# Two small matrix products of a two-layer graph kernel computed in column halves of the TensorE array

## The chip, the cores and the metric

The kernel runs on one core of one Trainium2 chip. A core has a matrix engine (TensorE, PE in the profile, with its weight loads shown apart as PEld), a vector engine (VectorE, DVE), a scalar engine (ScalarE, ACT), GpSimd (POOL) and a queue engine for transfers (SyncE, SP). TensorE writes its results to PSUM, the other operands lie in SBUF. The metric is the device time of the whole launch in microseconds (us), as the median of three runs; lower is better.

## What is computed

The input is a batch of eight graphs with 2048 nodes and 256 features each, and one adjacency matrix for all of them. Layer 0 is attention by chunks of 256 nodes with four heads of 64 features, in which every chunk has its own softmax; its output product (`ctx @ Wo.T`) goes through two residuals and two layer norms. Layer 1 is a graph attention whose values are the product of layer 0's result with `W`. The reference, cut:

```python
q = (x @ Wq.T + bq).reshape(B, N, H, Dh).transpose(0, 2, 1, 3)   # k, v likewise
scores = jnp.einsum('bhnd,bhjcd->bhnjc', q, kc) / sqrt(Dh)
scores = jnp.where(mask == 0, -10.0, jnp.clip(scores, -10.0, 10.0))
attn = jax.nn.softmax(scores, axis=-1)
ctx = jnp.einsum('bhnjc,bhjcd->bhnd', attn, vc)
out = layernorm(ctx @ Wo.T + bo + x) * gamma + beta
x = _layernorm(x + out)
...
Wh = (h @ W).reshape(B, N, N_H, D_F)
e = s_src[:, :, None, :] + s_dst[:, None, :, :]
e = jnp.where(mask, jnp.where(e > 0, e, 0.2 * e), -jnp.inf)
alpha = softmax(e, axis=2)
h_out = elu(jnp.einsum('bijh,bjhd->bihd', alpha, Wh))
x = _layernorm(x + h_out)
```

All matrix products of the layers are in float32.

## The kernel before

The graphs are worked through one after the other (`b` from 0 to 7), and the two layers are interleaved: while layer 0 of graph `b` is computed, layer 1 of graph `b - 1` runs beside it. The order of the instructions on every engine is the order in which the program issues them; nothing moves them later.

Layer 0 of a graph is cut into 64 slots (`SLOTS`). A slot is one group of 512 query nodes (`q`, four of them), one pair of heads (`hp`) and one chunk of keys (`c`). For TensorE a slot of the middle graphs is a fixed sequence:

- `scores` of the next slot (L388, tile `ps`): queries by keys, with 64 rows of the array for one head and the other 64 rows for the second, in the profile 64*128.
- `product(s, 0)` (L425, tile `pc`): probabilities by values for the first head. The 128 query nodes of a tile are cut into two halves of 64, `z` = 0 and 1, each of which takes 64 columns of the array and 64 partitions of PSUM, in the profile 128*64.
- `lower.step()` (L761, tile `pa`): two tiles of layer 1 of the graph before, cut the same way, 128*64.
- `product(s, 1)` (L425, tile `pc`): the second head.

A float32 matrix product shows as two records in the trace, each with a weight load of its own.

Class `Between` carries a group of 512 nodes from layer 0 to layer 1. Its `output` (L531, matmuls in L540, tile `po`) multiplies the attention result, which lies turned in `qT`, with `wo_sb`: for every tile of 128 nodes two matmuls, one for each half of the 256 inner features, with all 128 columns of the array, in the profile 128*128. Its `values` (L576, matmuls in L581, tile `pw`) multiplies the turned result of layer 0, `x1T`, with `w1_sb`, whose rows hold 256 values and eight attention terms, in the same way. DVE takes `po` from PSUM in `add` (L551), ACT takes `pw` in two copies (L588, L592). The steps between them are the norms on DVE, ACT and POOL.

Tables (`BEHIND`, `WIDE_BEHIND`, `LATER_BEHIND`) name the slots of a group behind which `output` and `values` are issued, with two tiles of nodes at a time: after `product(s, 1)`, and so before the next slot's `scores`. A graph has three groups in its slots, with two calls of `output` each and five calls of `values` together (the third group's second call falls behind the slots); the last of the five follows slot 63. The fourth group follows after the slots, at the change of layers: `order` is written out by hand there. For the first seven graphs it interleaves the group's steps with the projections of the next graph (L332 `pp`, L348 `pv`, 128*128) and the end of the third group's values, `before.values((2, 3))`. For the last graph there is no next one, and the steps stand between steps of layer 1 (`lower.step`). After that layer 1 of the last graph runs alone.

Other names in the views: `pr` (L399 on DVE, L411 on ACT) are the masked scores and their exponentials, `e` (L739, DVE) the attention weights of layer 1, `raw` (L432, ACT) the copy of `pc` out of PSUM, `pm` (L249) transposes of the mask in the first graph.

Of the kernel before, what the change touches and what calls it, by code (L numbers as in the profile page):

```python
# [17 lines left out]
P = 128  # L18
# [4 lines left out]
def adj_resnorm_kernel(  # L23
# [19 lines left out]
    nc = tc.nc  # L43
    B, N, F = x.shape
    H, D = a_src.shape
    NT = N // P
    NCH = N // CH
    KC = F // P
# [13 lines left out]

    SQ = 32
    QS = HP * NK
    SLOTS = NCH * QS
    UNITS = [(m, h) for m in range(len(BANKS)) for h in range(H)]
    FIRST = [sum(BANKS[:m]) for m in range(len(BANKS))]
# [51 lines left out]
    qT = big.tile([P, KC, N], F32, tag="qT", name="qT")  # L119
# [36 lines left out]
    wo_sb = weights(woT, "wo_sb")  # L156
# [5 lines left out]
    w1_sb = consts.tile([P, KC, F + 2 * H], F32, tag="w1_sb", name="w1_sb")  # L162
# [351 lines left out]
    class Between:  # L514
# [13 lines left out]
            row = beta_sb.unsqueeze(1).to_broadcast([P, QT, F])  # L528
            nc.vector.tensor_add(self.r, self.r, row)

        def output(self, us):  # L531
            n = len(us)
            if n == QT:
                po = two_banks([P, QT, F], "po")
            else:
                po = psM.tile([P, 2, F], F32, tag="psM", name="po")
            for k, u in enumerate(us):
                t = QT * self.g + u
                for c in range(KC):
                    nc.tensor.matmul(  # L540
                        po[:, k, :],
                        lhsT=qT[:, c, t * P : (t + 1) * P],
                        rhs=wo_sb[:, c, :],
                        start=(c == 0),
                        stop=(c == KC - 1),
                    )
            self.po = po

        def add(self, us):
# [23 lines left out]
        def turn_all(self):  # L573
            self.x1T = transposed(self.y, "x1T")

        def values(self, us):  # L576
            n, t = len(us), QT * self.g + us[0]
            pw = two_banks([P, n, CH], "pw")
            for k, u in enumerate(us):
                for c in range(KC):  # L580
                    nc.tensor.matmul(  # L581
                        pw[:, k, : F + 2 * H],
                        lhsT=self.x1T[:, c, u * P : (u + 1) * P],
                        rhs=w1_sb[:, c, :],
                        start=(c == 0),
                        stop=(c == KC - 1),
                    )
            nc.scalar.copy(  # L588
                self.waug[:, t : t + n, :, :D],
                pw[:, :, :F].rearrange("p k (h d) -> p k h d", h=H),  # L590
            )
            nc.scalar.copy(  # L592
                self.sd[:, :, t : t + n], pw[:, :, F : F + 2 * H].rearrange("p k x -> p x k")
            )
# [361 lines left out]
    for b in range(B):  # L956
        waug = blocks.tile([P, NT, H, D1], F32, tag="waug", name="waug")
        sd = small.tile([P, 2 * H, NT], F32, tag="sd", name="sd", bufs=1)
        if b == 0:
            for s in range(3):  # L960
                load_slab(s)
            scores(0)
            for u in range(KT):
                exps(0, u)
        if lower:
            for _ in range(STEP):
                lower.make()
        closing = Closing(b - 2, CLOSING) if b > 1 else None
        if closing:
            closing.do(-1)  # L970
        group = None
        for s in range(SLOTS):
            q, hp, c = where[s]
            i = s % QS
            send()
            if s + 3 < SLOTS:
                load_slab(s + 3)
            if i == 0:
                before = group
                group = Between(b, q - 1, sd, waug) if q else None  # L980
                wide = 0 < q < NCH - 1
                ahead = {} if wide else AHEAD
                if wide:
                    beside, behind = WIDE_BESIDE, WIDE_BEHIND
                else:
                    beside, behind = BESIDE if b else BESIDE_0, BEHIND
                later_beside, after = (LATER_BESIDE, LATER_BEHIND) if q > 1 else ({}, {})
            if before and later_beside and i in LATER_AHEAD:
                LATER_AHEAD[i](before)
            if i == 1 and q:  # L990
                load_context(b, q - 1, 1)
            if i == QS // 2 + 1:
                load_context(b, q, 0)
            if group and i in ahead:
                ahead[i](group)
            if s == SLOTS - 3 and b + 1 < B:
                turns = [project(b + 1, g) for g in range(NCH)]
                turns[0].pop(0)()
            if s:
                normalize(s - 1)  # L1000
            if s + 1 < SLOTS:
                scores(s + 1)

            if s == SLOTS - 1 and b + 1 < B:
                turns[0].pop(0)()
            if i == 3 and q:
                turn_context(q - 1, 1)
            if i == QS // 2 + (6 if wide else 3):
                turn_context(q, 0)
            if before and i in later_beside:  # L1010
                later_beside[i](before)
            if group:
                for step in beside.get(i, ()):
                    step(group)
            elif closing:
                closing.do(s, behind=False)
            product(s, 0)
            if s + 1 < SLOTS:
                for u in range(KT):
                    exps(s + 1, u)  # L1020
            if lower:
                if b + 1 < B or s < SLOTS - LATE:
                    lower.step()
            elif masks.left():
                masks.step()
            if not lower:
                product(s, 1, one_bank)
            elif b + 1 < B or s < SLOTS - LATE:
                product(s, 1)
            else:  # L1030
                product(s, 1, spare_bank)

            if before and i in after:
                after[i](before)
            if i == 0 and q:
                send_context(b, q - 1, 1)
            if i == QS // 2:
                send_context(b, q, 0)
            if group and i in behind:
                behind[i](group)  # L1040
            elif closing and not q:
                closing.do(s, beside=False)
        normalize(SLOTS - 1)

        send()
        before = group
        gd, fs = factors(b, sd, waug)
        group = None
        every = tuple(range(QT))

        def begin():
            nonlocal group
            group = Between(b, NCH - 1, sd, waug)

        def ctx():
            context(NCH - 1, 1)

        steps = [
            lambda: group.bias(),
            lambda: group.output(every),  # L1060
            lambda: group.add(every),
            lambda: (group.shift(), group.a.stats(every)),
            lambda: group.a.apply(group.y),
            lambda: (group.scale(), group.again(), group.b2.stats(every)),
            lambda: group.finish(),
            lambda: group.turn_all(),
            lambda: group.values((0, 1)),
            lambda: group.values((2, 3)),
        ]
        if b + 1 < B:  # L1070
            (k0, v0, q0), (l1, t1, k1, v1, q1), (l2, t2, k2, v2, q2), (l3, t3, k3, v3, q3) = turns
            rest = [lambda: lower.rest(1)] if lower else []
            order = [begin, *rest, l1, *rest, lambda: before.values((2, 3))]
            order += [*rest, ctx, *rest, *rest, k0]
            order += [steps[0], t1, steps[1], v0, steps[2], steps[3], l2, k1, steps[4], q0]
            order += [steps[5], v1, t2, l3, steps[6], q1, steps[7], k2, steps[8], steps[9], t3, v2]
            order += [lambda: [load_slab(s) for s in range(3)], fs[0], q2, fs[1], k3, fs[2], v3]
            order += [lambda: scores(0), q3, lambda: [exps(0, u) for u in range(KT)]]
        else:

            step = lower.step
            order = [begin, lambda: before.values((2, 3)), steps[0], step, ctx, step, steps[1], step]
            order += [steps[2], step, steps[3], step, steps[4], step, steps[5], step, steps[6], step]
            order += [steps[7], step, steps[8], step, steps[9], step, fs[0], step, fs[1], step, fs[2]]
            order += [step] * 5
            assert sum(p is step for p in order) == LATE
        for piece in order:
            send()
            piece()
        send()  # L1090
        undone = lower.tail if lower else []
        lower = Layer1(b, gd, waug)
        lower.tail += undone
# [57 lines left out]
```

## Time and profile before

| What | Value |
|---|---|
| Time, median of 3 runs | 3769.13 us |
| Lowest and highest run | 3766.95 and 3769.89 us |
| Span of the profiled execution, first to last instruction | 3764.9 us |
| Mean granted TensorE clock in it | 0.993 |
| `po` matmuls (L540): records, mean of one | 512, 391 ns |
| `pw` matmuls (L581): records, mean of one | 512, 398 ns |
| `pc` matmuls (L425): records, mean of one | 32768, 224 ns |
| `pa` matmuls (L761): records, mean of one | 32768, 224 ns |
| `ps` matmuls (L388): records, mean of one | 4096, 617 ns |

For the profiled execution the span is the only time there is; it lies 2.1 us below the lowest of the three runs. The duration of one matmul record covers its whole way through the array, while the next ones have already started: 32768 records of 224 ns would be 7.3 ms one after another. What a group of matmuls costs is therefore read from the start of its first record to the start of what follows it.

### The profile page before, as it was taken

To read this page: it belongs to the slowest core of one execution; us is meant where nothing else is said; L and a number is where in the kernel's file an instruction comes from. 1 tells how busy PE (TensorE), PEld (TensorE's weight loads), DVE (VectorE), ACT (ScalarE), POOL (GpSimd) and SP (SyncE) were. 2 spreads that over 40 slices of the span, in tenths; PEclk is the share of its full clock that TensorE was granted. 3 is DMA by queue.
4 is the path that set the end of the run, shared out by engine and by line. 5 is a ranking of instruction groups with operands and counts; after the bars stand their busy time and mean duration, and the time that the engine had idled before them with its cause. 6 is when DMAs were issued, how large, how long until landed. Compare 5 with 4: busy or idle time off the path is not lost.

```text
span 3764.9 us, 159631 instructions
## 1 busy us (share of the span) xinstructions
PE 3655.7 (97%) x72100; PEld 2743.7 (73%) x72100; DVE 3138.5 (83%) x4213; ACT 1979.9 (53%) x3571; POOL 1368.3 (36%) x1202
## 2 busy tenths in 40 slices
PE   9999999999999999999999999999999999999787
PEld 5656677776777777776777767777677777776676
DVE  5877589976999689995999959998699977997899
ACT  4666455555555555554555545555555555555322
POOL 1445234333433343333443324433343333334300
PEclk9999999999999999999999999999999999999899
DMA  6653334333333343333433334333433333332344
GB/s 164 152 117 70 80 96 109 105 75 112 109 105 105 86 123 100 104 96 89 133 99 94 101 93 133 106 104 76 113 109 105 105 82 115 111 98 73 100 150 137
DMA packets 672092, 398.46 MB, mean 106 GB/s; under 512 B 427312, under 2 KB 591536, under 8 KB 671408
## 3 DMA queue, kind: packets, MB, share of 16 engines
q1 hardware_dynamic: 621408, 354.55, 35.8%
q10 hardware_dynamic: 50000, 33.70, 2.8%
q8 instruction: 564, 9.24, 1.0%
q14 instruction: 120, 0.98, 0.1%
HBM read 331.22 MB, written 56.89 MB: 103 GB/s over the span
## 4 chain that ended last, share of the span: by engine, by line
PE 84%; DVE 7%; issue 4%; ACT 3%; DMA 1%; SPq 0%; ACTq 0%; POOL 0%; DVEq 0%; POOLq 0%
PE pc L425 25%; PE ps L388 23%; PE pa L761 21%; PE pp L332 5%; PE pw L581 3%; PE po L540 3%; DVE e L739 3%; PE pv L348 2%; DVE pr L399 2%; ACT y L505 1%; ACT pr L411 1%; DVE y L560 0%; DMA xp<-in_x_dram 0%; DVE y L557 0%; ACT qT L340 0%
## 5 line engine op out<-in xcount | busy, mean ns | idle before, releaser
L399 DVE SCALAR_TENSOR_TENSOR pr<-ps,slab 128x1024 f32<-128x1024 f32 x1024 | 1193.7, 1207 | 216.4 <-PE ps L388 212.6
L425 PEld LDWEIGHTS pc<-vaug,pr 128*64 128x64 f32 x32768 | 1038.7, 138 | 404.8 <-issue 298.4
L739 DVE SCALAR_TENSOR_TENSOR e<-srow,gd,et 128x1024 f32<-128x1024 f32 x1024 | 1277.4, 1291 | 14.8 <-PE pa L761 7.6
L425 PE MATMUL pc<-vaug,pr 128*64 128x65 f32 x32768 | 1153.6, 224 | 15.1 <-ACT pr L411 9.6
L761 PE MATMUL pa<-waug,e 128*64 128x65 f32 x32768 | 1070.1, 224 | 45.6 <-DVE e L739 41.4
L761 PEld LDWEIGHTS pa<-waug,e 128*64 128x64 f32 x32768 | 1016.4, 139 | 64.0 <-DVE e L739 55.5
L411 ACT ACTIVATE pr<-pr 128x1024 f32<-128x1024 f32 x1024 | 1040.3, 1055 | 39.7 <-DVE pr L399 30.8
L388 PE MATMUL ps<-qT,kT 64*128 64x512 f32 x4096 | 1024.7, 617 | 3.6 <-DVE pr L399 2.9
L432 ACT COPY raw<-pc 128x260 f32<-128x260 f32 x1024 | 381.3, 373 | 1203.1 <-PE pc L425 1176.4
L447 POOL TENSOR_TENSOR part<-raw,rd 128x512 f32<-128x512 f32 x448 | 468.6, 1046 | 1384.5 <-DVE rd L440 1370.1
L449 POOL TENSOR_TENSOR acc<-acc,part 128x512 f32<-128x512 f32 x448 | 575.3, 1284 | 35.2
L388 PEld LDWEIGHTS ps<-qT,kT 64*128 64x128 f32 x4096 | 347.8, 186 | 321.8 <-issue 201.4
L440 DVE RECIPROCAL rd<-raw 128x8 f32<-128x8 f32 x512 | 100.8, 197 | 120.0 <-ACT raw L432 118.8
L447 POOL TENSOR_TENSOR acc<-raw,rd 128x512 f32<-128x512 f32 x64 | 66.9, 1045 | 343.5 <-DVE rd L440 343.5
L793 ACT ACTIVATE sums<-sums,dn 128x64 f32<-128x64 f32 x504 | 131.9, 337 | 12.2 <-DVE dn L787 12.2
L500 POOL TENSOR_TENSOR rs_c<-rs_c,nhalf 128x4 f32<-128x4 f32 x32 | 52.7, 1647 | 232.5 <-DVE off_c L499 232.5
L581 PE MATMUL pw<-w_sb,x1T 128*128 128x264 f32 x512 | 128.0, 398 | 4.7 <-DVE x1T L294 4.7
L540 PE MATMUL po<-wo_sb,qT 128*128 128x256 f32 x512 | 126.2, 391 | 5.7 <-DVE qT L467 2.8
L332 PE MATMUL pp<-xT,wk_sb 128*128 128x512 f32 x256 | 119.2, 609 | 7.9 <-ACT qT L340 6.6
L332 PE MATMUL pp<-xT,wq_sb 128*128 128x512 f32 x256 | 116.2, 596 | 0.0
L348 PE MATMUL pv<-wv_sb,xT 128*128 128x256 f32 x512 | 115.9, 379 | 0.0
L581 PEld LDWEIGHTS pw<-w_sb,x1T 128*128 128x128 f32 x512 | 95.0, 192 | 25.0 <-DVE x1T L294 4.9
(103 smaller groups left out, 1843.7 us busy)
## 6 DMA issues: line engine op xcount, KB each, us to landing
et<-edgeD SPq DMA_DIRECT2D x512, 256.0 KB, 3.0
slab<-clipD SPq DMA_DIRECT2D x512, 128.0 KB, 3.1
srow<-rowD SPq DMA_DIRECT2D x64, 512.0 KB, 5.1
xg<-in_x_dram SPq DMA_DIRECT2D x32, 512.0 KB, 4.9
x1D<-y ACTq DMA_DIRECT2D x32, 512.0 KB, 3.9
x1g<-x1D SPq DMA_DIRECT2D x32, 512.0 KB, 5.1
out_dram<-o SPq DMA_DIRECT2D x30, 512.0 KB, 3.4
ctxD<-acc ACTq DMA_DIRECT2D x56, 256.0 KB, 2.6
```

Source lines behind the costliest of these rows:

```text
L332: nc.tensor.matmul(pps[c], lhsT=w[:, kc, c * P : (c + 1) * P], rhs=st["xT"][:, kc, :], start=(kc == 0), stop=(kc == KC - 1),)
L388: nc.tensor.matmul(ps[:, k, :], lhsT=kT[rows, hp, t * P : (t + 1) * P], rhs=qT[rows, hp, cols], start=True, stop=True,)
L399: nc.vector.scalar_tensor_tensor(pr, pss[u], -CLIP, slab[:, u, :].unsqueeze(1).to_broadcast([P, 2, CH]), op0=ALU.max, op1=ALU.min,)
L411: nc.scalar.activation(pr, pr, AF.Exp, scale=0.125)
L425: nc.tensor.matmul(pc[z * D : (z + 1) * D, i, :], lhsT=probs[s][u][:, k, i * P + z * D : i * P + (z + 1) * D], rhs=vaug[:, KT * c + u, 2 * ...
L432: nc.scalar.copy(raws[s][:, k], pc)
L447: nc.gpsimd.tensor_mul(part, raw[:, :, :, :D], rd.to_broadcast([P, 2, QT, D]))
L449: nc.gpsimd.tensor_add(accv, accv, part)
L540: nc.tensor.matmul(po[:, k, :], lhsT=qT[:, c, t * P : (t + 1) * P], rhs=wo_sb[:, c, :], start=(c == 0), stop=(c == KC - 1),)
L581: nc.tensor.matmul(pw[:, k, : F + 2 * H], lhsT=self.x1T[:, c, u * P : (u + 1) * P], rhs=w1_sb[:, c, :], start=(c == 0), stop=(c == KC - 1),)
L739: nc.vector.scalar_tensor_tensor(e[:, :w], self.rows[n][:, :w], self.gd[:, h, j : j + 1], self.edge[k // JG][:, j % JG, :w], op0=ALU.max, ...
L761: nc.tensor.matmul(self.pa[i // QT][z * D : (z + 1) * D, i % QT, :], lhsT=e[:, i * P + z * D : i * P + (z + 1) * D], rhs=self.waug[:, j, h ...
```

## The change

`output` and `values` get an argument `parts`, which is either `HALVES` (nodes 0 to 63 and 64 to 127 of a tile) or `WHOLE`. With `HALVES` every matmul becomes two, each with 64 columns of weights and 64 partitions of the result, and both with the same moving rows. The calls in the slots use the default, `HALVES`. At the change of layers the first seven graphs use `WHOLE`, the last graph `HALVES`.

```diff
+    HALVES = (slice(0, D), slice(D, P))
+    WHOLE = (slice(0, P),)
...
-        def output(self, us):
+        def output(self, us, parts=HALVES):
...
                 for c in range(KC):
-                    nc.tensor.matmul(
-                        po[:, k, :],
-                        lhsT=qT[:, c, t * P : (t + 1) * P],
-                        rhs=wo_sb[:, c, :],
-                        start=(c == 0),
-                        stop=(c == KC - 1),
-                    )
+                    for z in parts:
+                        nc.tensor.matmul(
+                            po[z, k, :],
+                            lhsT=qT[:, c, t * P + z.start : t * P + z.stop],
+                            rhs=wo_sb[:, c, :],
+                            start=(c == 0),
+                            stop=(c == KC - 1),
+                        )
...
-        def values(self, us):
+        def values(self, us, parts=HALVES):
...
-                    nc.tensor.matmul(
-                        pw[:, k, : F + 2 * H],
-                        lhsT=self.x1T[:, c, u * P : (u + 1) * P],
-                        rhs=w1_sb[:, c, :],
-                        start=(c == 0),
-                        stop=(c == KC - 1),
-                    )
+                    for z in parts:
+                        nc.tensor.matmul(
+                            pw[z, k, : F + 2 * H],
+                            lhsT=self.x1T[:, c, u * P + z.start : u * P + z.stop],
+                            rhs=w1_sb[:, c, :],
+                            start=(c == 0),
+                            stop=(c == KC - 1),
+                        )
...
+        parts = WHOLE if b + 1 < B else HALVES
+
         steps = [
             lambda: group.bias(),
-            lambda: group.output(every),
+            lambda: group.output(every, parts),
...
-            lambda: group.values((0, 1)),
-            lambda: group.values((2, 3)),
+            lambda: group.values((0, 1), parts),
+            lambda: group.values((2, 3), parts),
         ]
...
-            order = [begin, *rest, l1, *rest, lambda: before.values((2, 3))]
+            order = [begin, *rest, l1, *rest, lambda: before.values((2, 3), parts)]
...
-            order = [begin, lambda: before.values((2, 3)), steps[0], step, ctx, step, steps[1], step]
+            order = [begin, lambda: before.values((2, 3), parts), steps[0], step, ctx, step, steps[1], step]
```

## The prediction

> **What bounds the kernel now.** I read the page first, then the chain of waits, then the timeline of TensorE (PE) around one of the groups that are changed, and last the waits and the busy times by stretch, to see whether another engine stands ready to take its place.
>
> ```profile
> PE 3655.7 (97%) x72100; PEld 2743.7 (73%) x72100; DVE 3138.5 (83%) x4213; ACT 1979.9 (53%) x3571; POOL 1368.3 (36%) x1202
> PE 84%; DVE 7%; issue 4%; ACT 3%; DMA 1%; SPq 0%; ACTq 0%; POOL 0%; DVEq 0%; POOLq 0%
> ```
>
> A busy PE is not a PE at its peak, so the chain matters more: PE carries 84% of it. In the middle of the span, from 433 to 3405 us, the waits of PE (columns: total us, times, longest) come to 14 us over six graphs, with these ahead:
>
> ```profile
> PE pp L332 <- ACT qT L340: 5.7, 6, 0.9
> PE pc L425 <- ACT pr L411: 3.4, 7, 0.5
> PE pc L425 <- ACT raw L432: 2.9, 6, 0.5
> ```
>
> So what shortens PE's queue there shortens the run. The timeline of PE (start, us, what, how many) of slots with an output group and with a values group, and then without:
>
> ```profile
> 1554.15 2.04 PE L761 MATMUL pa<-waug,e 128*64 128x65 f32 x64
> 1556.01 1.10 PE L425 MATMUL pc<-vaug,pr 128*64 128x65 f32 x32
> 1557.05 1.99 PE L540 MATMUL po<-wo_sb,qT 128*128 128x256 f32 x8
> 1558.97 1.99 PE L388 MATMUL ps<-qT,kT 64*128 64x512 f32 x8
> 1560.89 1.15 PE L425 MATMUL pc<-vaug,pr 128*64 128x65 f32 x32
> 1561.87 2.04 PE L761 MATMUL pa<-waug,e 128*64 128x65 f32 x64
> 1563.74 1.10 PE L425 MATMUL pc<-vaug,pr 128*64 128x65 f32 x32
> 1564.77 2.05 PE L581 MATMUL pw<-w_sb,x1T 128*128 128x264 f32 x8
> 1566.75 1.99 PE L388 MATMUL ps<-qT,kT 64*128 64x512 f32 x8
> ```
>
> To be read from start to start. pa (128*64: the array cut in two column halves) takes 1556.01 - 1554.15 = 1.86 us for 64 records, 29 ns each, with pc of the same cut on both sides. 32 records of pc at that pace are 0.93 us; the pc ahead of po takes 1557.05 - 1556.01 = 1.04, so 0.11 us goes where the cut changes, and the pc that follows ps takes 0.98, 0.05 over its pace. po takes 1.92, pw 1.98. Narrow windows on one such group show where inside it (the row gives the first start in the window):
>
> ```profile
> 752.89 0.48 PE L540 MATMUL po<-wo_sb,qT 128*128 128x256 f32 x1
> 753.21 0.59 PE L540 MATMUL po<-wo_sb,qT 128*128 128x256 f32 x2
> 754.50 0.38 PE L540 MATMUL po<-wo_sb,qT 128*128 128x256 f32 x1
> 754.81 0.70 PE L388 MATMUL ps<-qT,kT 64*128 64x512 f32 x2
> 756.73 0.28 PE L425 MATMUL pc<-vaug,pr 128*64 128x65 f32 x2
> ```
>
> The second record starts 0.32 us after the first, the eighth six steps later: (754.50 - 753.21) / 6 = 0.215 us is the pace. So 0.32 - 0.215 = 0.105 us is the entry, and 754.81 - 754.50 - 0.215 = 0.095 us the way out into ps. The last two rows show two records of ps and two of pc starting within hundredths of a microsecond: halves of the array run at the same time from the first record on.
>
> **What the Trainium skill says.** TensorEngine Tiling (Array Packing), Key Properties: a change of the tiling mode, not merely of the tile, drains TensorE, and tiles load weights and multiply independently. The trace agrees: about 0.1 us at each change of cut, nothing between pa and pc. TensorE: Matmul & The Clock Gate, LDWEIGHTS (loading the stationary operand): a load costs its columns over 1.2 per ns, estimates of 107 ns for 128 columns and 53 for 64; the entries of 105 ns (po) and 50 ns (pc after ps) agree, so an entry is a first load that nothing hides. The same page, Why this matters for your kernels: three column tiles of 32 with 512 moving columns were 2.38 times as fast, not 3. In this trace two halves do better: 65 columns at po's rate would take 65/256 x 0.215 = 55 ns, and a pair of halves takes 2 x 29 = 58.
>
> **The change part by part.** Only PE's instructions change; each other engine has the same ones in the same order. An untiled record of 0.215 us becomes two records on the column halves, which stream the same rows of wo_sb or w1_sb. At equal pace and side by side, a pair takes 0.215 us, as long as the whole one did. So the streaming costs nothing more; what changes is the cut.
>
> Per group of eight in a slot, between pc and ps: the 0.105 us entry goes, since the first load of 64 columns can be made beside pc's last records, as it is between pc and pa; pc's way out, 0.095 us, goes; the way out into ps stays. Saved: 0.20 us. The pace of half records of 256 and 264 columns is in no row. Bounds: not below 0.215, since as many columns pass as before; at most 58/55 of that, 0.227, if what the 65-column pair loses is a share of its length, which would take 8 x 0.012 = 0.10 of the 0.20. I take 0.215: the row pairs of ps run 512 columns at (1558.97 to 1560.89, less 0.1 in and 0.1 out) 1.72/4 = 0.43 a pair, double po's 0.215, so what the 65-column pair adds looks fixed, and fixed it is 3 ns.
>
> How many: each graph has three groups of nodes with two output groups in slots and five values groups, 11 of them, 88 in all. In seven graphs the last (slot 63) is followed at once by the other half of its values, which stay whole: the change of cut only moves, 0.
>
> - Graphs 1 to 6: 10 x 6 x 0.20 = 12.0 us.
> - Graph 0: seven groups follow pc without a wait; one of these (159 us) and the one before it (151 us) are followed by slots where PE waits for DVE's share of the mask work, which takes the gain back. Six x 0.20, and 0.05 (a first load of 64 instead of 128 columns) for each of two that start after a wait: 1.3.
> - Graph 7: six groups before 3405 us at 0.20; later two without a wait at 0.20 and two after one at 0.05: 1.7.
> - Last change of layers: pw of slot 63 and the next (16 records), po (16), pw, pw (8 each), with 128*64 work on both sides, so that entry and both ways out go: 4 x (0.105 + 0.095 + 0.095) = 1.2. VectorE (DVE) makes e for that stage and is short of time there, but it waits for PE right behind these groups:
>
> ```profile
> 3510.50 1.28 DVE L739 SCALAR_TENSOR_TENSOR e<-srow,gd,et 128x1024 f32<-128x1024 f32 x1 [2.77 <-PE pa L761]
> 3539.09 1.28 DVE L739 SCALAR_TENSOR_TENSOR e<-srow,gd,et 128x1024 f32<-128x1024 f32 x1 [1.51 <-PE pa L761]
> ```
>
> Sum: 12.0 + 1.3 + 1.7 + 1.2 = 16.2 us. The profiled execution (3764.9) would have 3748.7. Its span lies 4.2 below the median of the runs, 3769.13; less 16.2 that is 3753.
>
> Is there room on DVE? Two slots of graph 3 and the whole of it, by stretch (length, then busy us of PE, PEld, DVE):
>
> ```profile
> 1330.00:1779.00 449.00, 446.73 (x8979) 337.43 (x8980) 382.72 (x512) 243.33 (x443) 171.34 (x151) 1.00 0.38 103
> 1497.10:1502.90 5.80, 5.80 (x140) 4.50 (x136) 5.80 (x7) 3.49 (x8) 2.33 (x2) 1.00 0.26 73
> 1673.20:1681.00 7.80, 7.80 (x149) 5.96 (x146) 7.39 (x8) 3.69 (x7) 3.78 (x5) 1.00 0.19 53
> ```
>
> DVE is full in plain slots behind the groups (5.80 of 5.80) and falls back by some tenths there, without stopping PE. It catches up in slots like the third, where it has at least 0.4 us to spare; 0.2 of that goes. In total it has 66 us to spare in 449. So it stays hidden, but not by much.
>
> **Rivals.**
>
> 1. *Half the gain* (12%): only one of the two costs goes, because the first load isn't made ahead over the change of shape, or DVE, short by 0.2 in each such slot, holds PE later. For: DVE's full slots. Against: pc to pa shows neither cost. About -8: 3761.
> 2. *Nothing* (7%): the halves of a matmul are started in order, so that the second half's last pass has no partner: one column time of 0.215 more in each group eats the 0.20. Against: pc's records start in pairs from the first. 3769.
> 3. *Slower* (7%): two halves that stream 256 columns from the same tile do not keep the pace. 186 node tiles are halved, 93 groups of eight. At the page's 2.38 of 3 a pair would take 0.215/0.79 = 0.272, 8 x 0.057 = 0.45 more per group: 93 x 0.45 = 42, less 16: 3795. With no overlap at all 93 x 1.72 = 160, less 16: 3913. It decides from 16.2/93/8 = 0.022 us more per pair, a pace of 0.237. Against: pa, 65 columns from one tile for both halves, at nearly full pace.
>
> **How the numbers follow.** The forecast, faster by 13 to 19 us (3750 to 3756), has 74%, the rivals 12, 7 and 7. The granted clock is 0.98 from 3405 to 3497 us and 0.91 from 3545 on, where PE pauses, and these dips will fall at other moments; I add a microsecond below and some three above rival 1's 3761: 3749 to 3764. A measurement of this kernel can tell 0.2%, 7.5 us, from no change: faster by more than that holds the forecast and most of rival 1, 0.84; within it 0.08; slower 0.08.
>
> **What would show it.** The step from po's first record to ps should be about 1.82 us, with pc ahead of it 0.93; pairs of po at 0.215; the sum of PE's waits for DVE in 433 to 3405 us still near nothing. A pair pace above 0.237, or new waits of pc or pa for DVE, would make it wrong.

## The result and the profile after

The changed kernel takes 3752.01 us in the median of five runs (3751.16 to 3757.13), the kernel before 3769.13 (3766.95 to 3771.0): 17.1 us less. The ratio is 0.9957, 95% interval 0.9945 to 0.9969, so it is faster by 0.31 to 0.55%. The span of the profiled execution went from 3764.9 to 3751.5 us, by 13.4; the profiled execution of before lay 4.2 us below its median, that of after 0.5, which is the rest of the 17.

The page after, its first row and the chain by engine:

```profile
PE 3637.1 (97%) x72844; PEld 2699.4 (72%) x72844; DVE 3139.9 (84%) x4213; ACT 1978.7 (53%) x3571; POOL 1366.8 (36%) x1202
PE 84%; DVE 7%; issue 3%; ACT 3%; DMA 1%; SPq 1%; ACTq 0%; POOL 0%; DVEq 0%; POOLq 0%
```

PE runs 744 records more and is busy for 18.6 us less. The rest stayed: PE still carries 84% of the chain, and DVE's busy time differs by 1.4 us. The timeline of PE in the two slots that were shown of before, one with an output group and one with a values group (lines of the code have moved by two to four: L427 is `pc`, L543 `po`, L585 `pw`, L765 `pa`, L390 `ps`; the window ends inside the last row):

```profile
1551.56 2.04 PE L765 MATMUL pa<-waug,e 128*64 128x65 f32 x64
1553.43 1.10 PE L427 MATMUL pc<-vaug,pr 128*64 128x65 f32 x32
1554.36 1.90 PE L543 MATMUL po<-wo_sb,qT 128*64 128x256 f32 x16
1556.19 1.99 PE L390 MATMUL ps<-qT,kT 64*128 64x512 f32 x8
1558.11 1.15 PE L427 MATMUL pc<-vaug,pr 128*64 128x65 f32 x32
1559.09 2.04 PE L765 MATMUL pa<-waug,e 128*64 128x65 f32 x64
1560.96 1.10 PE L427 MATMUL pc<-vaug,pr 128*64 128x65 f32 x32
1561.89 1.95 PE L585 MATMUL pw<-w_sb,x1T 128*64 128x264 f32 x16
1563.77 1.56 PE L390 MATMUL ps<-qT,kT 64*128 64x512 f32 x6
```

The pc ahead of po is down from 1.04 to 0.93 us, start to start: the way out of its cut is gone. po is down from 1.92 to 1.83, pw from 1.98 to 1.88: the first load is hidden, the way out into ps is still there. Together 0.20 us a group. A graph in which PE meets no other disturbance takes 446.56 us, from its first `ps` to that of the next, where it took 448.52: 1.96 us less for ten groups, 0.196 each. Two narrow windows on one group show the pairs:

```profile
1450.58 0.39 PE L543 MATMUL po<-wo_sb,qT 128*64 128x256 f32 x2
1452.09 0.39 PE L543 MATMUL po<-wo_sb,qT 128*64 128x256 f32 x2
```

Two records start together, and the last pair starts seven steps after the first: (1452.09 - 1450.58) / 7 = 0.216 us a pair, against 0.215 for one whole record before; at two decimals of a microsecond the views don't tell these two apart.

### The profile page after: what moved, and what is told of

The parts are those of the page before. It is cut to its first block, busy times and chain, and to the rows that moved or that the text cites. A ratio compares the mean times of both kernels' runs of the same rounds, so it can differ in the third digit from the quotient of the medians.

```text
span 3751.5 us, 161119 instructions
## 1 busy us (share of the span) xinstructions
PE 3637.1 (97%) x72844; PEld 2699.4 (72%) x72844; DVE 3139.9 (84%) x4213; ACT 1978.7 (53%) x3571; POOL 1366.8 (36%) x1202
## 4 chain that ended last, share of the span: by engine, by line
PE 84%; DVE 7%; issue 3%; ACT 3%; DMA 1%; SPq 1%; ACTq 0%; POOL 0%; DVEq 0%; POOLq 0%
PE pc L427 25%; PE ps L390 23%; PE pa L765 22%; PE pp L334 5%; PE pw L585 3%; PE po L543 3%; DVE e L743 2%; PE pv L350 2%; DVE pr L401 2%; ACT y L507 1%; ACT pr L413 1%; SPq L284 1%; DMA xp<-in_x_dram 0%; DVE y L563 0%; DVE y L560 0%
## 5 line engine op out<-in xcount | busy, mean ns | idle before, releaser
L427 PEld LDWEIGHTS pc<-vaug,pr 128*64 128x64 f32 x32768 | 1038.6, 138 | 405.4 <-issue 299.0
L427 PE MATMUL pc<-vaug,pr 128*64 128x65 f32 x32768 | 1153.4, 224 | 15.7 <-ACT pr L413 9.6
L765 PE MATMUL pa<-waug,e 128*64 128x65 f32 x32768 | 1068.9, 224 | 47.9 <-DVE e L743 43.3
L765 PEld LDWEIGHTS pa<-waug,e 128*64 128x64 f32 x32768 | 1015.5, 139 | 65.7 <-DVE e L743 55.9
L390 PE MATMUL ps<-qT,kT 64*128 64x512 f32 x4096 | 1023.8, 616 | 3.9 <-DVE pr L401 3.2
L390 PEld LDWEIGHTS ps<-qT,kT 64*128 64x128 f32 x4096 | 347.0, 185 | 325.7 <-issue 200.8
L585 PE MATMUL pw<-w_sb,x1T 128*64 128x264 f32 (+1 forms) x856 | 125.4, 392 | 5.7 <-DVE x1T L296 5.7
L543 PE MATMUL po<-wo_sb,qT 128*64 128x256 f32 (+1 forms) x912 | 120.9, 380 | 6.2 <-DVE qT L469 3.4
L296 DVE STREAM_TRANSPOSE xT<-xp 128x1024 f32<-128x1024 f32 x28 | 34.8, 1244 | 92.0 <-PE pw L585 77.8
```

What stands on the lines that cost most here:

```text
L390: nc.tensor.matmul(ps[:, k, :], lhsT=kT[rows, hp, t * P : (t + 1) * P], rhs=qT[rows, hp, cols], start=True, stop=True,)
L427: nc.tensor.matmul(pc[z * D : (z + 1) * D, i, :], lhsT=probs[s][u][:, k, i * P + z * D : i * P + (z + 1) * D], rhs=vaug[:, KT * c + u, 2 * ...
L543: nc.tensor.matmul(po[z, k, :], lhsT=qT[:, c, t * P + z.start : t * P + z.stop], rhs=wo_sb[:, c, :], start=(c == 0), stop=(c == KC - 1),)
L585: nc.tensor.matmul(pw[z, k, : F + 2 * H], lhsT=self.x1T[:, c, u * P + z.start : u * P + z.stop], rhs=w1_sb[:, c, :], start=(c == 0), stop= ...
L765: nc.tensor.matmul(self.pa[i // QT][z * D : (z + 1) * D, i % QT, :], lhsT=e[:, i * P + z * D : i * P + (z + 1) * D], rhs=self.waug[:, j, h ...
```

## The experiments

Theory: what was saved is the change of cut, that is the drain and the first weight load that nothing hides; streaming costs nothing more or less. Rivals: halves are quicker in themselves; or finer parts are better; or another engine sets how much of the gain arrives. Times are medians; ratios are against the kernel before on the same chip. The runs below were made on several chips, where the median of before is 3769.2 to 3770.2 us, so a difference between two medians of different versions is uncertain by a microsecond or more; what decides is the traces, in which the steps of undisturbed graphs repeat within hundredths of a microsecond.

**Halves where the neighbours are whole.** The first seven graphs use halves at the change of layers too, where po and pw stand between pp and pv.

```diff
-        parts = WHOLE if b + 1 < B else HALVES
+        parts = HALVES
```

> Halves also at the change of layers of the first seven graphs, where the neighbours of po and pw are pp and pv, 128*128. Theory (only the change of cut counts): each of the two inner groups per graph now has a change of cut on both sides that was not there, so the step from the last pp over po to the first pv grows from 3.88 to about 4.1 us, and pv's first record by 0.1: some 0.35 x 14 = 5 us, 3757. Rival (halves are faster in themselves, since loads of 64 columns hide better): these groups get shorter too, by about 0.2 each, 3749.

Measured: 3757.92 us, ratio 0.9969 (0.9959 to 0.9979), 5.9 us above the changed kernel, whose interval this one overlaps. PE's timeline of this run at one change, then the same place in the changed kernel:

```profile
830.80 3.60 PE L334 MATMUL pp<-xT,wk_sb 128*128 128x512 f32 x8
834.33 3.67 PE L543 MATMUL po<-wo_sb,qT 128*64 128x256 f32 x32
837.93 3.72 PE L350 MATMUL pv<-wv_sb,xT 128*128 128x256 f32 x16
841.49 3.60 PE L334 MATMUL pp<-xT,wk_sb 128*128 128x512 f32 x8
```

```profile
832.19 3.60 PE L334 MATMUL pp<-xT,wk_sb 128*128 128x512 f32 x8
835.62 3.62 PE L543 MATMUL po<-wo_sb,qT 128*128 128x256 f32 x16
839.08 3.62 PE L350 MATMUL pv<-wv_sb,xT 128*128 128x256 f32 x16
842.53 3.60 PE L334 MATMUL pp<-xT,wk_sb 128*128 128x512 f32 x8
```

Start to start, pp, po and pv take 3.53, 3.60 and 3.56 us with halves, and 3.43, 3.46 and 3.45 whole: 0.35 us more, spread over the three as the theory has it. The same edit that saves 0.20 us between pc and ps costs 0.35 between pp and pv. There are two such groups in a graph; an undisturbed graph takes 447.21 us here and 446.56 in the changed kernel, 0.65 more. The first rival falls: its sign is wrong.

**Quarters.** The same change with four parts of 32 nodes.

```diff
-    HALVES = (slice(0, D), slice(D, P))
+    HALVES = tuple(slice(z, z + 32) for z in range(0, P, 32))
```

> The same change with four parts of 32 nodes in place of two of 64. Theory: 128*32 is another cut than the 128*64 of pc and pa, so the drain of 0.095 us is back and only the entry is shorter (a load of 32 columns in place of 128): pc to ps takes about 2.0 us for po, against 1.88 with halves and 2.08 whole, 3761 to 3764. Rival A (finer parts are good in themselves): 3752 or less. Rival B (four streams do not keep the pace): a group longer than 2.08 us, slower than before.

Measured: 3764.42 us, ratio 0.9985 (0.9978 to 0.9992), 0.4 us over what was expected. The timeline, and two narrow windows on this group of po (the row gives the first start among the records under way in the window):

```profile
1453.01 1.10 PE L427 MATMUL pc<-vaug,pr 128*64 128x65 f32 x32
1454.04 1.93 PE L543 MATMUL po<-wo_sb,qT 128*32 128x256 f32 x32
1455.91 1.99 PE L390 MATMUL ps<-qT,kT 64*128 64x512 f32 x8
```

```profile
1454.28 0.40 PE L543 MATMUL po<-wo_sb,qT 128*32 128x256 f32 x4
1455.58 0.40 PE L543 MATMUL po<-wo_sb,qT 128*32 128x256 f32 x4
```

pc is back at 1.03 us: its way out is there again. pc and po together take 2.90, against 2.76 with halves and 2.96 whole. The second four quarters start 0.24 us after the first (1454.28 - 1454.04), and from there to the last four are six steps: (1455.58 - 1454.28) / 6 = 0.217 us. So the quarters keep the pace of a whole record, and the entry is 0.24 - 0.217, some 0.025 us. With the entries of the prediction that makes 0.105, 0.05 and 0.025 us for 128, 64 and 32 columns: the entry goes with the columns of the first load, and the way out does not. It isn't fineness that pays; it is having the neighbour's cut.

**The order of the halves.** The loop over halves stands outside the one over the inner parts.

```diff
-                for c in range(KC):
-                    for z in parts:
+                for z in parts:
+                    for c in range(KC):
```

> The loops over halves and over the two inner parts are swapped: both matmuls of the first half are issued, then both of the second. Theory (matmuls start in the order of issue, but one that goes to other columns starts as soon as the one ahead has started): within a group every second one still finds a partner, but the last matmul of a group has none, so a group grows by two column times, 0.43 us, from 1.88 to 2.3, and the kernel by some 36 us, 3788. Rival (each half has its own queue, the order of issue does not count): 1.88 as before, 3752.

Measured: 3759.79 us, ratio 0.9975 (0.9966 to 0.9984), 7.8 us above the changed kernel. The theory of this run fell. Timeline, and a narrow window at the start of the group:

```profile
1450.25 1.10 PE L427 MATMUL pc<-vaug,pr 128*64 128x65 f32 x32
1451.19 1.95 PE L543 MATMUL po<-wo_sb,qT 128*64 128x256 f32 x16
1453.06 1.99 PE L390 MATMUL ps<-qT,kT 64*128 64x512 f32 x8
```

```profile
1451.19 0.44 PE L543 MATMUL po<-wo_sb,qT 128*64 128x256 f32 x2
```

po grew by 0.04 to 0.05 us, not by 0.43, and two records still start together, although two matmuls of the first half are issued ahead of the second half's. Both cannot be the first half's, since its columns are taken for 0.215 us by each; so the second half starts past a matmul of the first that is ahead of it. Over the 80 groups between pc and ps 0.05 us is 4 us. The rest, as far as the two profiled executions show it (8.5 us apart), is not the order of the halves: PE pauses for 2.8 us before the context's transposes (`pt`), for GpSimd, in two graphs, where the changed kernel has other pauses of 1.25 us; and the granted clock is 0.50 for 3.4 us on an output group of graph 7, where the changed kernel has 1.00, which costs some 1.6:

```profile
3431.80:3435.20 3.40, 3.40 (x16) 1.65 (x14) 0.00 (x0) 0.00 (x0) 2.10 (x2) 0.50 0.00 0
```

(Length, then busy us and records of PE, PEld, DVE, ACT and POOL; the third number from the end is the clock.) The pauses for GpSimd come and go: they are 0.2 us in the run with halves everywhere and 1.6 us in the last run below.

**One part alone.** Only the outputs in halves, then only the values (the edit: `parts=WHOLE` as the default of the other function, and `parts` dropped from its calls).

> Only the output products in halves, the values whole everywhere. Theory: 0.196 us for each of 48 groups in slots less what graph 0 takes back, and 0.3 in the last change: about 9 us less than before, 3760; pc to ps over po 1.88, over pw 2.13. Rival (the two parts help each other, or DVE is the bound once PE is shorter): a gain nearer 5 or nearer the whole 17.

> Only the values in halves, the output products whole everywhere. Theory: 0.196 us for each of 32 groups in slots between pc and ps, 0 for those behind slot 63 of seven graphs, three groups in the last change: about 7 us less than before, 3762; with the run of outputs alone it sums to the whole change's 17. Rival as there: the two do not add up.

Measured: 3759.81 us, ratio 0.9973 (0.9964 to 0.9982), and 3761.17, ratio 0.9978 (0.9968 to 0.9988): 10.4 and 8.6 us below the runs of before on their chips, 19.0 together, against 17.1 for the whole change. They add up within what such medians tell (the whole change's interval is 9 us wide). The traces say it more sharply: an undisturbed graph takes 447.34 us with the outputs alone and 447.73 with the values alone, 1.18 and 0.79 less than before, and the whole change saves 1.96. So nothing is held back by DVE when both are there. In the outputs-only run both kinds of group stand in the same trace:

```profile
1551.73 1.10 PE L427 MATMUL pc<-vaug,pr 128*64 128x65 f32 x32
1552.66 1.90 PE L543 MATMUL po<-wo_sb,qT 128*64 128x256 f32 x16
1554.49 1.99 PE L390 MATMUL ps<-qT,kT 64*128 64x512 f32 x8
...
1559.26 1.10 PE L427 MATMUL pc<-vaug,pr 128*64 128x65 f32 x32
1560.29 2.05 PE L585 MATMUL pw<-w_sb,x1T 128*128 128x264 f32 x8
1562.27 1.99 PE L390 MATMUL ps<-qT,kT 64*128 64x512 f32 x8
```

pc and po take 0.93 + 1.83, pc and pw 1.03 + 1.98.

**The same cost at another place.** In graph 0 the transposes of the mask (`pm`, 128*128) stand between the two pc of a slot. On top of the change, the whole step of the mask is issued behind the second one, right ahead of ps: the transposes, what DVE and ACT do with them, and the transfers that the step starts.

```diff
-            elif masks.left():
-                masks.step()
...
                 product(s, 1, spare_bank)
+            if not lower and masks.left():
+                masks.step()
```

> On top of the change, the transposes of the mask in graph 0 (pm, 128*128), which stand between the two pc of a slot, are issued behind the second pc, right ahead of ps. Theory: pc, pm, pc, ps has three changes of cut, pc, pc, pm, ps has two, so each of the 37 slots not held by DVE loses one way out and one entry of 64 columns, 0.095 + 0.05: about 5 us less than the changed kernel, 3747. Rival (in graph 0 DVE and ACT set the pace, and a later pm makes them later): no gain, or some us more.

Measured: 3741.77 us, ratio 0.9925 (0.9912 to 0.9939): 10.2 us below the changed kernel, and with the next run the fastest version of all. PE's timeline in a plain slot of this run, then of the changed kernel:

```profile
100.92 1.99 PE L390 MATMUL ps<-qT,kT 64*128 64x512 f32 x8
102.84 2.09 PE L427 MATMUL pc<-vaug,pr 128*64 128x65 f32 x64
104.86 0.45 PE L251 MATMUL pm<-identb,ab 128*128 128x128 bf16 x5
105.24 1.99 PE L390 MATMUL ps<-qT,kT 64*128 64x512 f32 x8
```

```profile
100.89 1.99 PE L390 MATMUL ps<-qT,kT 64*128 64x512 f32 x8
102.81 1.15 PE L427 MATMUL pc<-vaug,pr 128*64 128x65 f32 x32
103.89 0.45 PE L251 MATMUL pm<-identb,ab 128*128 128x128 bf16 x5
104.28 1.15 PE L427 MATMUL pc<-vaug,pr 128*64 128x65 f32 x32
105.36 1.99 PE L390 MATMUL ps<-qT,kT 64*128 64x512 f32 x8
```

A slot takes 4.32 us in place of 4.47: 0.15, the 0.095 + 0.05 expected. But over 37 slots that would be 5.6 us (in the trace some 20 slots show it, 3 us), and the run gained nearly twice as much.

**The masks taken apart.** pm stays between the two pc; the rest of the step is issued behind the second pc: what DVE and ACT do with it (`clip`, `edge`, and the next conversion) and the transfers, that is the stores of finished masks and the load of the next piece.

```diff
+        def early(self):
+            if self.bits:
+                t, m, ab = self.bits.pop(0)
+                self.held = (t, m, self.transposes(m, ab))
...
             elif masks.left():
-                masks.step()
+                masks.early()
...
                 product(s, 1, spare_bank)
+            if not lower and masks.left():
+                masks.step()
```

> Takes the run with the masks behind apart: the transposes of the mask stay between the two pc of the slot, as in the changed kernel, but what DVE and ACT do with them (clip, edge) and the next conversion stand behind the copy of the second pc. Theory (two effects): plain slots of graph 0 go back to 4.47 us, since pm is again between two pc, while the slots from 140 to 240 us keep what the masks-behind run gained, about 5 us, since raw no longer stands behind edge on ACT; 3746 or 3747. Rival (all of it came from the cut): 3752, as the changed kernel.

Measured: 3741.97 us, ratio 0.9925 (0.9911 to 0.9938), as fast as the run before it. Plain slots are at 4.47 us again, as expected. The gain, expected at 5 us, is 10: it lies where a group's norm steps and the mask work fall together. The changed kernel there, then this run:

```profile
180.56 1.15 PE L427 MATMUL pc<-vaug,pr 128*64 128x65 f32 x32
181.92 0.44 PE L251 MATMUL pm<-identb,ab 128*128 128x128 bf16 x5 [0.21 <-ACT edge L255]
182.29 1.15 PE L427 MATMUL pc<-vaug,pr 128*64 128x65 f32 x32
183.63 2.26 PE L390 MATMUL ps<-qT,kT 64*128 64x512 f32 x8 [0.19 <-DVE pr L401]
```

```profile
181.09 1.99 PE L406 MATMUL ps<-qT,kT 64*128 64x512 f32 x8
183.01 1.15 PE L443 MATMUL pc<-vaug,pr 128*64 128x65 f32 x32
184.10 0.51 PE L260 MATMUL pm<-identb,ab 128*128 128x128 bf16 x6
184.54 1.15 PE L443 MATMUL pc<-vaug,pr 128*64 128x65 f32 x32
```

In the first, pm waits for ACT to have emptied pm's bank and ps for DVE; in the second PE goes through. PE's own waits between 60 and 250 us are 11.2 us in the changed kernel, 6.6 in the masks-behind run and 5.5 here. From the slot that starts at 165.24 us in the changed kernel to the one at 246.74 the masks-behind run is 7.6 us quicker and this one 8.0, though it lacks the cut's share: there the two effects do not add. So the masks-behind run mostly gained from the order of the other work, and the cut's 0.15 us a slot shows only in the plain slots. Which part of that order it is stays open. The expectation named `raw` standing behind `edge` on ACT; but DVE's waits for `raw` between 60 and 240 us are 30.7 us in the changed kernel, 19.1 here and 4.9 in the masks-behind run, which is no faster for it.

## Why the prediction was right

The predicted 3753 lies 1 us from the median. The mechanism and the price of a group are as forecast; in the sum graph 0 is off by 2.0 us one way and graph 7 by 1.6 the other. Step by step, with the profiled executions of before and after:

- *What bounds the kernel.* Right. PE's waits between 433 and 3405 us are the same rows with the same numbers to 0.1 us, but for two short pauses, and none of them is for DVE.
- *The price of a group*, 0.20 us: the fences above give 0.11 + 0.09 for po and 0.10 + 0.10 for pw. The pace of a pair is 0.216 us, the lower of the two bounds; the price is right, and the runs with halves between whole neighbours and with quarters show that it is the change of cut. The records of the weight loads themselves last longer than the prediction's estimates of 107 and 53 ns: 190 ns for 128 columns, 137 for 64 and 109 for 32. They differ by 53 and 28 ns, as the entries do; some 83 ns are in each of them, and no group pays for these.
- *Graphs 1 to 6.* Predicted 12.0. From the first `ps` of graph 1 to that of graph 7 the runs draw apart by 10.9 us (starts 433.07 and 3124.59 before, 433.75 and 3114.35 after). Of the missing 1.1, pauses of PE in graphs 1 and 3, of 0.45 and 0.80, are 1.25, less one of 0.36 that before had; the rest is a price of 0.196 in place of 0.20. In graph 1 the steps of `pa` take 734.41 - 732.09 = 2.32 us in place of 1.87, and nothing in the profile releases it.
- *Graph 0.* Predicted 1.3 less, measured 0.7 more. The groups themselves brought 1.3, as reckoned. But 0.4 was lost before the first of them (the second slot starts at 69.0 before and 69.4 after). Some of it was taken back, as said, though not in the slots right behind the first two groups: 0.5 went in the one at 232 us, where PE waits 0.98 us for `edge` in place of 0.45. Then 1.1 was lost at the change of layers, where PE waits 5.66 us for `x1T` in place of 4.75. DVE makes `x1T` right behind the turned input of the next graph, for whose load (`xp`) it waits 4.69 in place of 3.77. No term of the prediction covers the start and the load.
- *Graph 7.* Predicted 1.7, measured 3.3: 1.2 from the six groups before 3405 us and 0.4 from two later ones, as reckoned, and 1.7 from the two that start after a wait, for which 0.1 was set. That is the clock. In both kernels PE waits 2.1 us for `raw` ahead of the first of these (L540 before, L543 after). Before, the clock then fell to half over this group and the slot behind it; after, it did not. The stretch of before, then the one of after that holds the same place in the code:

```profile
3437.00:3441.00 4.00, 4.00 (x12) 2.09 (x12) 0.10 (x1) 0.00 (x0) 1.89 (x2) 0.57 0.02 4
```

```profile
3426.00:3441.00 15.00, 12.12 (x180) 7.73 (x178) 7.19 (x12) 5.30 (x8) 4.07 (x5) 1.00 0.07 19
```

- *The last change.* Predicted 1.2, measured 1.2: DVE's `top`, just behind the four groups, starts at 3544.28 before and 3529.59 after, 14.7 apart, where the last `pc` of the slots, 3495.38 and 3481.87, were 13.5 apart. What the prediction left out is that layer 1 of the last graph, alone, gives it back. DVE's wait there for the attention row, before and after:

```profile
3571.08 2.48 DVE L739 SCALAR_TENSOR_TENSOR e<-srow,gd,et 128x1024 f32<-128x1024 f32 x2 [2.49 <-DMA srow<-rowD]
```

```profile
3556.61 2.48 DVE L743 SCALAR_TENSOR_TENSOR e<-srow,gd,et 128x1024 f32<-128x1024 f32 x2 [3.43 <-DMA srow<-rowD]
```

DVE comes to it earlier and waits longer, so 0.2 is lost by here. 1.0 more goes after it, 0.7 of that while the clock is at half for 6.8 us in place of 3.4; that the clock is the cause there was not shown. At the end the two are 13.4 apart.

For the profiled execution the sum was therefore 2.8 us too high, 16.2 for 13.4, and nearly all of that is in terms beside the price of a group. It would have been 4.4 too high without the dip of the clock that before happened to have in graph 7. The nearness of the median, 17.1, is in part luck: runs of one kernel differ by 4 to 6 us, and no median of the experiments can tell 16 from 17.

The rivals: "half the gain" fell because both costs are gone in the timeline, 0.10 us each, and the two parts add up with no new wait for DVE; "nothing" fell because the last pair of a group still starts together; "slower" fell with the pace of a pair, 0.216 against the 0.237 at which it would have begun.

## What to carry to other kernels

When PE is the bound, look at what it costs to pass from one group of matmuls to the next: start of the first record to start of the next group, less records times pace. Each change of how the array is cut cost about 0.1 us of drain and the first weight load (0.1 us at 128 columns, 0.05 at 64) here, so a small group should take the cut of its neighbours, even if that doubles its instructions, and should keep its own where the neighbours are uncut. And on an engine that works in order, look at what a copy stands behind: issuing the copies and transfers of the mask a little later in graph 0 brought 10 us more, without one instruction less.

## What the runs showed of the hardware

- Two halves of the array took 256 moving columns each, from the same tile, in the time of one whole record: 0.216 us a pair against 0.215, and four quarters did so in 0.217. The Trainium skill, TensorE: Matmul & The Clock Gate, Why this matters for your kernels, has a speedup of 2.38 for three column tiles; two and four tiles in a long row of matmuls lost under 1% here.
- Leaving a cut cost some 0.1 us at every change that was measured here, and the first load of the new one 0.105, 0.05 and 0.025 us for 128, 64 and 32 columns. Between neighbours of the same cut neither was paid.
- The two halves do not start strictly in the order of issue (third experiment). The same page of the Trainium skill, Part 3, The mechanism, has matmuls in strict order of start and end; the runs here show the second half starting past a matmul of the first, at a cost of 0.05 us a group. So what is said of the kernel before, that the order on every engine is that of issue, does not hold for the starts of these halves.
- The granted clock fell to half for 3.4 or 6.8 us behind waits of PE, at moments that differ from kernel to kernel: behind the same wait of 2.1 us in graph 7 it fell in the kernel before and in the third experiment, and not in the changed kernel. That alone moved a stage by 1.6 us, so a difference of 1 or 2 us in this kernel should not be explained before the clock has been looked at.
